# Two row tiles per visit in layer 1, and a reload in five parts

## The chip, the cores and the metric

The kernel runs on one core of one Trainium2 chip. The metric is the time of one execution on the device in microseconds (us), the median of several runs. A profile is one further execution, recorded instruction by instruction.

The core has engines that run side by side and wait for one another through semaphores. In the profile PE is the matrix array (PEld its weight loads), DVE the vector engine, ACT the scalar engine, POOL the general-purpose engine, and SP the engine that here only issues DMA transfers.

## The reference

Two layers of a graph network on 2708 nodes with 256 features. Layer 0 (top-p attention, two steps of neighbour averaging) is not touched by the change, except for where its result is kept. Layer 1 is graph attention with four heads of 64 features, followed by a residual and a layer norm:

```python
x = _layernorm(x + _L0_gnn_ref(x, adj, ...), axis=-1)
...
Wh = jnp.einsum('nd,hdo->nho', x, W)
s_i = jnp.einsum('nho,ho->nh', Wh, a_src)
s_j = jnp.einsum('nho,ho->nh', Wh, a_dst)
e = jax.nn.leaky_relu(s_i[:, None, :] + s_j[None, :, :], NEG_SLOPE)
adj_sl = adj.at[idx, idx].set(1.0)
mask = (adj_sl != 0)[:, :, None]
attention = jax.nn.softmax(jnp.where(mask, e, -jnp.inf), axis=1)
h_prime = jnp.einsum('ijh,jho->iho', attention, Wh)
x = _layernorm(x + h_prime.reshape(n, h * fo), axis=-1)
```

## The kernel before

The 2708 rows are cut into 22 row tiles: 16 of 128 rows and 6 of 110. Layer 1 takes its target rows in three groups (`spans`): tiles 0 to 7, 8 to 15, and 16 to 21. For each group it runs over all 22 source tiles, two at a time; `i` below is the place of a source tile in its group, 0 to 21, and `n` its place in the whole run of 66.

For one source tile and one group there are these steps.

- `mask` (line 245, by way of `neighbours` and `bars`): SP loads a block of the transposed adjacency matrix, 512 KB for a group of 1024 targets; ACT turns it into zeros and ones with Sign and Square (lines 247 and 248). DVE sets the diagonal where the source tile belongs to the group (line 251). Three such blocks are held. Within group 0 it also loads the source tile's values `v` (line 1594).
- `weights` (line 1606): for each of the four heads one DVE operation makes the unnormalised attention weights `pt` out of the targets' factors, the source's factor and the mask. There are three sets of `pt` (`DEEP`).
- `values` (line 1618) and `denominators` (line 1628): PE sums the weighted values and the weights themselves into PSUM. The array is split into four column strips of 32 (`SIDE`), so that four products run beside each other. The result stands transposed: features down, target rows across.

Two source tiles are summed together: values of both, then denominators of both. When a group is through, its sums are copied to `val` and `den`, and its tiles are put on the list `rest`. During the next group `beside(g, i)`, called before the values of each pair (even `i`) and again between values and denominators (odd `i`), takes work from that list. `settle` is a generator for one row tile. Its first step transposes the two halves of `val` and the denominators back with three full-array transposes into a PSUM tile `aux` (lines 1532 and 1533), takes the reciprocal on DVE (line 1535), and scales the four heads on ACT (line 1549). A later step adds the layer's input `xe` on POOL (line 1554). Then follow the layer norm on ACT and POOL (`layernorm_beside`, lines 149 to 157) and the store (line 1572, issued by ACT). `aux` has two buffers. Other users of `aux` are `share` (line 212), which turns the next group's target factors, at `i` = 11; `prepared` and `sources`, which finish the last three row tiles of layer 0 during group 0; and `verdict`, a test of layer 0's approximations whose sum (line 1481) falls into group 1. Group 2 is settled in `closing`, at the end.

`share` and `spread` send the factors through memory: SP stores one line (line 217, `shared<-line`), waits for it, and reads it back four times spread over all partitions (line 225, `r<-shared`).

Layer 0 writes its finished rows to memory (`xd`) as it goes, 19 tiles of them. The array `xe` in SBUF, in which layer 0 held something else, gets them back in group 0 of layer 1: at `i` = 12 POOL writes one column of all 19 tiles (line 1710), which SP's transfers wait for, and SP issues one transfer of 2 MB for tiles 0 to 15 and one of 330 KB for tiles 16 to 18 (line 1712). They are needed by the POOL adds of groups 1 and 2.

The order of PE, ACT, DVE and POOL in layer 1 is that of the program text. SP's order is left to the scheduler, which places each transfer by its own estimate.

```python
            if fast and (g, i) == (0, 12):
                nc.gpsimd.memset(xe[:, 0 : NT - LATE, 0:1], 0.0)
                for t0, t1 in ((0, 16), (16, NT - LATE)):
                    nc.sync.dma_start(
                        xe[: rows[t0], t0:t1, 0:D], xd[: rows[t0], t0:t1, :]
                    )
            if rest and i >= 2 and i % 2 == 0:
                running.append(settle(*rest.pop(0)[:4], aux(), False))
                next(running[-1])
```

Of the kernel before, what the change touches and what calls it, by code (L numbers as in the profile page):

```python
# [45 lines left out]
def kernel(  # L46
# [16 lines left out]
    nc = tc.nc  # L63
    N, D = x.shape
    DA = w1T.shape[1]
    STEPS = u1T.shape[0]
    H, _, FO = gat_w.shape
    DC = D // P
    NT = (N + P - 1) // P

    rows = [P] * 16 + [110] * 6
# [31 lines left out]
    xe = const.tile([P, NT, D + 2], F32, name="xe")  # L103
# [12 lines left out]
    xd = kept.tile([P, NT, D], F32, name="xd")  # L116
# [4 lines left out]
    LATE = 3  # L121
# [23 lines left out]
    def layernorm_beside(dst, src, m):  # L145

        col = {k: small.tile([P, 1], F32, name=f"lb_{k}")[:m] for k in ("nm", "sq", "rs", "nb")}
        nm, sq, rs, nb = col.values()
        nc.scalar.activation(dst, src, AF.Copy, accum_out=sq)
        nc.gpsimd.tensor_scalar(nm, sq, -1.0 / D, None, op0=ALU.mult)  # L150
        yield
        nc.scalar.activation(dst, src, AF.Square, bias=nm, accum_out=sq)
        nc.gpsimd.tensor_scalar(sq, sq, 1.0 / D, LN_EPS, op0=ALU.mult, op1=ALU.add)
        nc.gpsimd.tensor_tensor(rs, sq, minus_half[:m], op=ALU.pow)
        nc.gpsimd.tensor_mul(nb, nm, rs)
        yield
        nc.scalar.activation(dst, src, AF.Identity, scale=rs, bias=nb)
# [50 lines left out]
    def share(g, tr):  # L208

        span, m = spans[g], rows[spans[g][0]]  # L210
        k = len(span) * H
        nc.tensor.transpose(
            tr[:k, 0, :m],
            s_src[:m, span[0] : span[-1] + 1, :].rearrange("p t h -> p (t h)"), ident[:m, :m],
        )
        nc.scalar.activation(line[:k, :m], tr[:k, 0, :m], AF.Exp, scale=1.0 - NEG_SLOPE)
        nc.sync.dma_start(shared[g], line[:k, :m])

    def spread(g, r):

        lines = shared[g].rearrange("(t h) m -> h t m", h=H)
        n = len(spans[g]) * rows[spans[g][0]]
        for k in range(2):
            for h in range(2):
                nc.sync.dma_start(
                    r[k][:, h, :n].rearrange("p (t m) -> p t m", t=len(spans[g])),
                    lines[2 * k + h].partition_broadcast(P),
                )
# [25 lines left out]
    def room(pool):  # L254

        return [
            pool.tile([P, N], F32, name="e")[:, : 2 * GW].rearrange("p (h i) -> p h i", h=2)
            for _ in range(2)
        ]
# [1236 lines left out]
    def layer1(ep, adjp, r=None, verdict=None, early=()):  # L1496
# [27 lines left out]
        def aux():  # L1524
            return ps_u.tile([P, H, P], F32, name="aux")

        def settle(g, t, val, den, u, last):

            m = rows[t]
            cols = slice(off[t] - off[spans[g][0]], off[t + 1] - off[spans[g][0]])  # L1530
            for q in range(2):
                nc.tensor.transpose(u[:m, q, :], val[:, q, cols], ident)  # L1532
            nc.tensor.transpose(u[:m, 2, :], den[:, cols], ident)  # L1533
            rden = small.tile([P, H], F32, name="rden")
            nc.vector.reciprocal(  # L1535
                rden[:m], u[:m, 2, :].rearrange("p (h o) -> p h o", h=H)[:, :, 0]
            )
            res = pp.tile([P, H, FO], F32, name="res", bufs=5)
            sums = u[:m, 0:2, :].rearrange("p q (h o) -> p (q h) o", h=2)
            flat = res[:m].rearrange("p h o -> p (h o)")  # L1540
            if last and t % 2:
                for h in range(H):
                    nc.vector.scalar_tensor_tensor(  # L1543
                        res[:m, h, :], sums[:, h, :], rden[:m, h : h + 1],
                        xe[:m, t, h * FO : (h + 1) * FO], op0=ALU.mult, op1=ALU.add,
                    )
            else:
                for h in range(H):
                    nc.scalar.activation(
                        res[:m, h, :], sums[:, h, :], AF.Copy, scale=rden[:m, h : h + 1]  # L1550
                    )
            yield
            if not (last and t % 2):
                nc.gpsimd.tensor_add(flat, flat, xe[:m, t, 0:D])
                yield
            o = pp.tile([P, D], F32, name="o")[:m]
            if last:
                st = small.tile([P, 6], F32, name="ln_st")[:m]
                mv = small.tile([P, 2], F32, name="ln_mv")[:m]
                ve, rs, nb = (small.tile([P, 1], F32, name=f"ln_{k}")[:m] for k in ("ve", "rs", "nb"))  # L1560
                nc.vector.bn_stats(st, flat)  # L1561
                nc.vector.bn_aggr(mv, st)  # L1562
                nc.vector.tensor_scalar(ve, mv[:, 1:2], LN_EPS, None, op0=ALU.add)  # L1563
                nc.gpsimd.tensor_tensor(rs, ve, minus_half[:m], op=ALU.pow)  # L1564
                nc.gpsimd.tensor_scalar(nb, mv[:, 0:1], rs, -1.0, op0=ALU.mult, op1=ALU.mult)
                yield
                nc.scalar.activation(o, flat, AF.Identity, scale=rs, bias=nb)  # L1567
                nc.sync.dma_start(out[off[t] : off[t + 1], :], o)
                return
            yield from layernorm_beside(o, flat, m)  # L1570
            yield
            nc.scalar.dma_start(out[off[t] : off[t + 1], :], o)

        fast = r is not None
# [9 lines left out]
        for span in spans:  # L1584
            gw = off[span[-1] + 1] - off[span[0]]
            part = CHUNK if span is not spans[-1] else len(span) // 2 * rows[span[0]]
# [103 lines left out]
            yield from sources(t, pp, aux, nc.scalar)  # L1690


        late = []
        if verdict:
            late += [[2 * k, prepared(NT - LATE + k)] for k in range(LATE)]
            late.append([NT + 4, verdict(aux)])
        rest, running = [], []

        def beside(g, i):

            for part in list(late):
                if part[0] > 0:
                    part[0] -= 1
                elif next(part[1], late) is late:
                    late.remove(part)
            for part in list(running):
                if next(part, running) is running:
                    running.remove(part)
            if fast and (g, i) == (0, 12):
                nc.gpsimd.memset(xe[:, 0 : NT - LATE, 0:1], 0.0)  # L1710
                for t0, t1 in ((0, 16), (16, NT - LATE)):
                    nc.sync.dma_start(
                        xe[: rows[t0], t0:t1, 0:D], xd[: rows[t0], t0:t1, :]
                    )
            if rest and i >= 2 and i % 2 == 0:
                running.append(settle(*rest.pop(0)[:4], aux(), False))
                next(running[-1])
            if i == NT // 2 and g + 1 < len(spans):
                share(g + 1, aux())
                if g % 2:  # L1720
                    targets[g + 1] = room(ep)
                else:
                    targets[g + 1] = [rp.tile([P, 2, GW], F32, name=f"r{q}") for q in range(2)]
                spread(g + 1, targets[g + 1])
# [6 lines left out]
        for n in range(0, len(order), 2):  # L1731
            g, i, j = order[n]
            beside(g, i)
            weights(n + 2)
            mask(n + 3)
# [19 lines left out]
            if not last:  # L1755
                beside(g, i + 1)
# [3 lines left out]
            if last:  # L1760
# [4 lines left out]
                rest = [(g, t, val, den) for t in spans[g]]  # L1765
# [6 lines left out]
    with ExitStack() as both:  # L1772

        adjp = both.enter_context(tc.tile_pool(name="adjp", bufs=3))
        ep = both.enter_context(tc.tile_pool(name="ep", bufs=3))
        left = fast_layer0(ep, adjp)
        with tc.manual_schedule(engines=engines):
            layer1(ep, adjp, *left)
    flag = nc.values_load(bad[0:1, 0:1])
    with tc.If(flag > 0):  # L1780
        general_layer0()
        with ExitStack() as again:
            adjp = again.enter_context(tc.tile_pool(name="adjp", bufs=3))
            ep = again.enter_context(tc.tile_pool(name="ep", bufs=3))
            layer1(ep, adjp)
# [45 lines left out]
```

## Time and profile before

| | us |
|---|---|
| median of 3 runs | 1533.94 |
| lowest, highest | 1533.94, 1536.61 |
| profiled execution | 1534.79 |
| its span, first to last instruction | 1532.7 |
| PE busy over the span | 1492.8 |
| DVE busy | 1277.1 |
| ACT busy | 804.9 |
| POOL busy | 594.5 |

Layer 1 takes roughly the last 350 us. In a timeline a row gives the start and the length in us, the engine, the line, the operation with what it writes and reads, its shape and how many of them were put together; what stands in brackets is the idle time ahead of the row and what ended it. A PE row's length is modelled, so distances between starts say more than lengths. In a table of stretches each row gives a stretch, its length, the busy time (and number of instructions) of PE, PEld, DVE, ACT and POOL, the granted clock of PE, the busy share of the DMA engines, and GB/s.

### The profile page before, as it was taken

The page shows a single profiled execution, that of the slowest core. Times are in us where ns is not written, and L with a number is a line of the kernel's source. Part 1 is how long each engine was busy: PE and PEld are TensorE (multiplying, and loading weights), DVE is VectorE, ACT ScalarE, POOL GpSimd, SP SyncE. Part 2 cuts the span into 40 slices and gives each one's busy share as a digit, 9 for nine tenths or more (in the row PEclk, how much of TensorE's full clock was granted, in tenths as well). Part 3 has the DMA queues.
Part 4 walks back from the last instruction along what each step waited for, and adds up shares of the span by engine and source line. Part 5 has one row for each costly group of instructions (what it writes and reads, how often), then busy time and mean ns, then how long its engine had stood idle before and what let it go on. Part 6 is the DMA issues. An engine that isn't in the chain of part 4 may idle for free. (4 is left out here: it accounts for less than half of the span.)

```text
span 1532.7 us, 29967 instructions
## 1 busy us (share of the span) xinstructions
PE 1492.8 (97%) x10537; PEld 1064.6 (69%) x10537; DVE 1277.1 (83%) x3749; ACT 804.9 (53%) x1495; POOL 594.5 (39%) x959
## 2 busy tenths in 40 slices
PE   8999999999999999999999999999999999999996
PEld 4477777776778889988988888887898223433343
DVE  3699888999714978888889898989895998999996
ACT  3444444444326556655655666666653344456474
POOL 0046657566013323323454554544444310035143
PEclk9999999999999999999999999999999999999998
DMA  6288888878037755554564555555455355334331
GB/s 166 66 246 277 247 247 281 266 234 255 12 102 235 211 165 167 161 162 137 159 199 142 165 183 170 182 166 178 137 151 178 109 172 167 100 104 135 88 105 53
DMA packets 214488, 255.97 MB, mean 167 GB/s; under 512 B 42145, under 2 KB 180541, under 8 KB 214329
## 3 DMA queue, kind: packets, MB, share of 16 engines
q1 hardware_dynamic: 205622, 246.62, 53.7%
q10 hardware_dynamic: 8707, 7.35, 1.5%
q8 instruction: 85, 1.39, 0.4%
q14 instruction: 74, 0.61, 0.1%
HBM read 190.10 MB, written 62.44 MB: 165 GB/s over the span
## 5 line engine op out<-in xcount | busy, mean ns | idle before, releaser
L816 ACT ACTIVATE junk<-e,minus,rth 128x2708 bf16<-128x2708 f32 (+1 forms) x88 | 232.9, 2646 | 52.5 <-POOL rth L848 51.7
L271 ACT COPY eT<-tr 128x512 f32<-128x512 f32 (+5 forms) x264 | 141.5, 536 | 199.0 <-PE tr L266 196.5
L284 PE MATMUL att<-xm,eT 128*128 128x256 f32 (+3 forms) x968 | 230.8, 379 | 0.3 <-ACT xa L1325 0.3
L284 PE MATMUL att<-ba,eT 128*128 128x256 f32 (+3 forms) x968 | 230.9, 379 | 0.0
L1618 PE MATMUL acc<-pt,v 128*32 128x512 f32 (+3 forms) x2112 | 222.9, 543 | 2.1 <-DVE pt L1606 1.1
L1606 DVE SCALAR_TENSOR_TENSOR pt<-e,tj,blk 128x1024 f32<-128x1024 f32 (+3 forms) x176 | 186.6, 1125 | 8.3 <-ACT xw L1265 5.4
L284 PEld LDWEIGHTS att<-xm,eT 128*128 128x128 f32 (+3 forms) x968 | 169.6, 186 | 22.0 <-ACT xa L1325 0.7
L284 PEld LDWEIGHTS att<-ba,eT 128*128 128x128 f32 (+3 forms) x968 | 169.5, 186 | 22.0 <-ACT eT L271 0.8
L795 ACT ACTIVATE e<-lg 128x1024 f32<-128x1024 f32 (+1 forms) x132 | 121.0, 921 | 105.7 <-PE lg L791 102.2
L1109 PE MATMUL walk<-xe,blk 128*128 128x128 f32 (+3 forms) x1386 | 172.9, 275 | 1.2 <-ACT xw L1123 0.7
L1109 PEld LDWEIGHTS walk<-xe,blk 128*128 128x128 f32 (+1 forms) x1386 | 164.4, 187 | 11.4 <-issue 7.4
L1618 PEld LDWEIGHTS acc<-pt,v 128*32 128x32 f32 (+1 forms) x2112 | 73.4, 109 | 130.8 <-issue 76.2
L266 PE MATMUL tr<-ident,e 128*128 128x128 f32 (+3 forms) x968 | 147.5, 271 | 4.8 <-ACT eT L271 4.8
L266 PEld LDWEIGHTS tr<-ident,e 128*128 128x128 f32 (+3 forms) x968 | 111.3, 139 | 47.1 <-issue 26.7
L1109 PE MATMUL walk<-xm,blk 128*128 128x128 f32 (+3 forms) x1034 | 131.3, 277 | 5.4 <-DVE u_sb L1119 2.9
L1109 PEld LDWEIGHTS walk<-xm,blk 128*128 128x128 f32 (+3 forms) x1034 | 124.2, 188 | 14.0 <-issue 6.1
L1628 PE MATMUL acc<-pt,sb 128*32 128x512 f32 (+3 forms) x1056 | 115.7, 542 | 0.0
L1606 DVE SCALAR_TENSOR_TENSOR pt<-r,tj,blk 128x1024 f32<-128x1024 f32 (+1 forms) x88 | 109.9, 1312 | 1.3 <-issue 0.6
L247 ACT ACTIVATE blk<-blk 128x1024 f32<-128x1024 f32 (+3 forms) x66 | 63.3, 960 | 82.5 <-DMA blk<-in_adjT_dram 76.2
L896 DVE MAX8 cand<-e 128x8 f32<-128x170 f32 (+1 forms) x352 | 85.9, 320 | 21.1 <-ACT e L795 21.0
L896 DVE MAX8 cand<-scr 128x8 f32<-128x97 f32 (+1 forms) x616 | 102.8, 244 | 0.0
L914 DVE MAX8 top<-work 128x8 f32<-128x128 f32 (+3 forms) x242 | 82.3, 340 | 8.3
(283 smaller groups left out, 2410.2 us busy)
## 6 DMA issues: line engine op xcount, KB each, us to landing
blk<-in_adjT_dram SPq DMA_DIRECT2D x68, 512.0 KB
blk<-S SPq DMA_DIRECT2D x48, 512.0 KB
blk<-D SPq DMA_DIRECT2D x24, 512.0 KB
blk<-in_adjT_dram SPq DMA_DIRECT2D x26, 440.0 KB
D<-blk SPq DMA_DIRECT2D x16, 512.0 KB
S<-scr SPq DMA_DIRECT2D x16, 512.0 KB
S<-blk SPq DMA_DIRECT2D x16, 512.0 KB
xm<-S SPq DMA_DIRECT2D x16, 512.0 KB
```

The lines of the kernel that those rows point to most:

```text
L247: nc.scalar.activation(bar, bar, AF.Sign)
L266: nc.tensor.transpose(tr[: rows[t], q, :m], e[:m, off[t] : off[t + 1]], ident[:m, :m])
L271: copy(eT[:k, : len(grp), :m], tr[:k, : len(grp), :m])
L284: nc.tensor.matmul(acc, eT[: rows[t], q, :m], value(t), start=(t == 0), stop=(t == NT - 1),)
L795: nc.scalar.activation(halves[:m, :, c0 : c0 + w], lg[:m, :, :w], AF.Exp, accum_out=zp[:m, n : n + 1],)
L816: nc.scalar.activation(junk[:m], e[:m], func, scale=rth, bias=minus1[:m], accum_out=acc)
L896: nc.vector.max(cand[:, n, :], src[:m, n * size : min(N, (n + 1) * size)])
L914: nc.vector.max(top[:, k : k + 8], work if k else flat)
L1109: nc.tensor.matmul(ac, blk[:k, j, :], MOVING[name](j, k, w), start=start and j == 0, stop=j == PAIRS - 1, skip_group_check=True,)
L1606: nc.vector.scalar_tensor_tensor(pt[:k, :gw], targets[g][h // 2][:k, h % 2, :gw], tj[:k, j, h : h + 1], bar, op0=ALU.max, op1=ALU.mult,)
L1618: nc.tensor.matmul(acc[h // 2][c][to : to + SIDE, :w], v[j][:k, h, o : o + SIDE], probs[n][h][:k, c0 : c0 + w], **at,)
L1628: nc.tensor.matmul(acc[2][c][h * SIDE : (h + 1) * SIDE, :w], sb[:k, j, h : h + 1].to_broadcast([k, SIDE]), probs[n][h][:k, c0 : c0 + w], **at,
```

## The change

Two things are changed in `beside`. The reload of `xe` is cut into five parts, each with its own POOL write, placed at `i` = 12, 14, 16, 18 and 19 of group 0. And a visit for transposes takes two tiles from `rest` at `i` = 2, 6, 10 and 14, both with their own `aux` buffer, where before it took one at each even `i` from 2 to 16.

```diff
+        BACK = {12: (0, 4), 14: (4, 8), 16: (8, 12), 18: (12, 16), 19: (16, NT - LATE)}
         late = []
...
-            if fast and (g, i) == (0, 12):
-                nc.gpsimd.memset(xe[:, 0 : NT - LATE, 0:1], 0.0)
-                for t0, t1 in ((0, 16), (16, NT - LATE)):
-                    nc.sync.dma_start(
-                        xe[: rows[t0], t0:t1, 0:D], xd[: rows[t0], t0:t1, :]
-                    )
-            if rest and i >= 2 and i % 2 == 0:
-                running.append(settle(*rest.pop(0)[:4], aux(), False))
-                next(running[-1])
+            if fast and g == 0 and i in BACK:
+                t0, t1 = BACK[i]
+                nc.gpsimd.memset(xe[:, t0:t1, 0:1], 0.0)
+                nc.sync.dma_start(xe[: rows[t0], t0:t1, 0:D], xd[: rows[t0], t0:t1, :])
+            if rest and i % 4 == 2:
+                both = [settle(*rest.pop(0)[:4], aux(), False) for _ in rest[:2]]
+                for part in both:
+                    next(part)
+                running.extend(both)
```

## The prediction

> **What bounds the kernel now.** I read the page's engine table, then stretches of layer 1 (busy time of each engine), the timelines of PE, DVE, SP and ACT there, and the chain of waits. Layer 1 is 1186 us to the end. Its three groups of targets hold PE and DVE nearly full; two stretches (groups 1 and 2, closing left out) by PE, PEld, DVE, ACT, POOL:
>
> ```profile
> 1315.90:1435.23 119.33, 119.19 (x1086) 37.01 (x1082) 114.89 (x128) 65.89 (x122) 40.51 (x40) 1.00 0.39 111
> 1435.23:1507.80 72.57, 72.50 (x986) 33.69 (x982) 71.18 (x94) 48.12 (x111) 22.97 (x39) 1.00 0.35 96
> ```
>
> A PE that waits in its queue still counts as busy, so the period of a pair of source tiles tells more than the share. The PE timeline, start and length, with a visit (three transposes, L1532 and L1533) and without:
>
> ```profile
> 1393.39 7.07 PE L1618 MATMUL acc<-pt,v 128*32 128x512 f32 x64
> ...
> 1403.83 0.44 PE L1532 MATMUL aux<-ident,val 128*128 128x128 f32 x2
> 1404.10 0.27 PE L1533 MATMUL aux<-ident,den 128*128 128x128 f32 x1
> 1404.30 7.07 PE L1618 MATMUL acc<-pt,v 110*32 110x512 f32 x64
> ...
> 1414.63 7.05 PE L1618 MATMUL acc<-pt,v 110*32 110x512 f32 x64
> ```
>
> A pair with a visit takes 1404.30 - 1393.39 = 10.91 us, one without 10.33: the constant lengths show PE setting the pace in group 1. A visit costs 0.60 (10.91 less 10.31, the mean of the last pairs). In group 2 the same reading gives 7.29 and 6.70 (1494.43 to 1501.13). How much lies in the tiles and how much in going in and out shows where three tiles are turned in one visit, in the closing:
>
> ```profile
> 1514.99 0.43 PE L1532 MATMUL acc<-ident,val 128*110 128x128 f32 x2
> 1515.26 0.27 PE L1533 MATMUL acc<-ident,den 128*110 128x128 f32 x1
> 1515.37 0.38 PE L1532 MATMUL acc<-ident,val 128*110 128x128 f32 x2
> 1515.59 0.27 PE L1533 MATMUL acc<-ident,den 128*110 128x128 f32 x1
> 1515.69 0.38 PE L1532 MATMUL acc<-ident,val 128*110 128x128 f32 x2
> ```
>
> The second tile starts 0.38 after the first, the third 0.32 after the second (1515.69 - 1515.37). DVE is close behind in group 2; four masked products (L1606), reciprocal, four, four:
>
> ```profile
> 1456.56 3.74 DVE L1606 SCALAR_TENSOR_TENSOR pt<-e,tj,blk 128x660 f32<-128x660 f32 x4 [0.17 <-issue]
> 1460.22 0.17 DVE L1535 RECIPROCAL rden<-aux 128x4 f32<-128x4 f32 x1
> 1460.31 3.32 DVE L1606 SCALAR_TENSOR_TENSOR pt<-e,tj,blk 128x660 f32<-128x660 f32 x4
> 1463.84 3.84 DVE L1606 SCALAR_TENSOR_TENSOR pt<-e,tj,blk 128x660 f32<-128x660 f32 x4 [0.21 <-issue]
> ```
>
> DVE idles 0.2 in a period of 7.28, until the last denominators of the pair give their buffers back. From 1482 on the chain of waits leaves PE for DVE. The other half of the change is on SP. In group 0 one mask comes late:
>
> ```profile
> 1249.10 0.38 SPq L1712 DMA_DIRECT2D xe<-xd  x1
> 1252.23 0.33 SPq L245 DMA_DIRECT2D blk<-in_adjT_dram  x1
> 1252.61 0.38 SPq L1712 DMA_DIRECT2D xe<-xd  x1
> 1257.41 0.33 SPq L245 DMA_DIRECT2D blk<-in_adjT_dram  x1
> 1257.83 0.38 SPq L217 DMA_DIRECT2D shared<-line  x1
> 1263.07 6.37 SPq L225 DMA_DIRECT2D r<-shared  x4
> 1277.60 1.06 ACT L247 ACTIVATE blk<-blk 128x1024 f32<-128x1024 f32 x1 [8.14 <-DMA blk<-in_adjT_dram]
> 1280.03 1.14 PE L171 MATMUL aux<-wx,xT 128*110 128x264 f32 x4 [1.81 <-ACT xT L167]
> ```
>
> Behind it on ACT stands a copy (L167) that PE needs, and PE loses 1.81.
>
> **What the Trainium skill says.** "TensorEngine Tiling (Array Packing)", Key Properties: changing the tiling mode drains the array. The trace agrees: the sums run 128x32, the transposes 128x128, and 0.28 of a visit's 0.60 isn't transposes. "SBUF — State Buffer", SBUF: two separate sides: a DVE operation with two inputs in SBUF and a GpSimd operation that reads SBUF shut each other out. Here too: single products last 1.27, but 1.76 beside POOL's add (L1554). "DMA: Bandwidth & Descriptors", Queues, rings and completion order: a ring's descriptors are taken in order. The trace fits: the 16 KB of shared<-line, issued at 1257.83, held L225 until 1263.07, behind some 3.4 MB.
>
> **The change part by part.** *Visits.* Eight settled tiles in group 1 and eight in group 2 went out at i = 2, 4, ... 16; now two each at i = 2, 6, 10, 14. Eight visits vanish; their 24 transposes stay, at 0.11 each, 0.33 a tile (the closing's 0.32 rounded up).
> - Group 1: 4 x (0.60 - 0.33) = 1.1 off, if DVE keeps up. When PE reaches a product, DVE had it ready early; the smallest lead for the second tile of a pair (its third head) falls to 1.7 at i = 12. PE gains at most 0.83 on that point, so DVE stays ahead.
> - Group 2: 4 x (0.59 - 0.33) = 1.0 off PE. Two pairs take 14.31 instead of 14.57; DVE needs 2 x 7.08 = 14.2. It just holds, but two adds on POOL now fall into one pair: 2 x 0.48 on one pair's products eat half of a lead of 1.8. I charge 0.15 once, 0 to 0.5. At the end, where DVE leads, one L1554 add less stands beside it (the add of the visit at i = 16 hit 1501.00, 3.75 instead of 3.36): 0.2 back, 0 to 0.4.
> - New wait: both aux buffers are taken at once. At i = 11 of group 1 the verdict (L1481) and share (L212) want them back. Before, the reciprocal came at 1376.58, four activations (L1549, 0.93) ended at 1377.72, and PE arrived at 1378.11. Now eight end 0.93 later, 1378.65, less what DVE gains by then (0.28 by PE's start, 0.35 by an add moved): and 0.1 more for the second reciprocal: about 1378.1, with L212 due at 1378.0 (1378.23 - 0.55 for two visits saved + 0.33 for the double one). Behind it on PE stand that pair's denominators. I charge 0.2; 0 to 0.8.
> - ACT: eight activations in a row put the next mask back by 0.93. In group 2 it is ready some 6.2 after the pair's start, and DVE wants it at 6.8: nothing, but 0.3 a visit (1.2 in all) if ACT is later by 0.9. Reciprocals, adds, statistics and output DMAs are as many as before, in twos; o has two buffers, both DMAs leave one step before reuse, as now: nothing.
>
> *Reload.* By the instruction order of the changed kernel, POOL's five memsets stand back to back, none with a wait. SP isn't ordered by hand: its order becomes three parts, mask, two parts, mask, shared, four r, mask. So the reload is not spread over eight source tiles: it goes out as early as before. The same 2.4 MB and two masks lie ahead of shared, the same four r ahead of the late mask. Three issues more, 3 x 0.38 = 1.1 us, fall into SP's idle time (1249.5 to 1252.2, 1253 to 1257.4); four memsets of 0.13 at most follow the first, while POOL has 83 us free. The first of the two masks lands some 1.5 us earlier (512 KB less ahead at 350 GB/s, what the stretch from 1251 to 1257 moved): nobody waits, since DVE runs without a gap there. Cost 0; between -1.4 (the late mask in time) and +1.5 (SP held by r longer).
>
> Sum: -1.1 - 1.0 + 0.15 - 0.2 + 0.2 = -1.95, say -2.0. Profiled execution: 1534.79 (span 1532.7 and 2.1 around it) to 1532.8. It lies 0.85 over the median of the runs; taken from the median, 1533.94 - 2.0 = 1531.9.
>
> **Rivals.** (A) The late mask comes in time after all. For: it is the largest stall of layer 1, and smaller parts let something between. Against: shared waits behind the same bytes, r behind shared. Pair i = 14 would take 11.99 like pair 12, not 13.42: -1.4 more, -3.4, 1530.5.
> (B) DVE takes over. For: 71.18 of 72.57 us busy in group 2, from 1482 on the chain. Against: its idle 0.2 per pair is real. Group 2 gives nothing, group 1 half: -0.5, 1533.4.
> (C) Slower: r held up. In the instruction order each transfer waits for an earlier one that used the same of eight completion semaphores, and each r now waits for a smaller mask or reload part; if these finish after shared has landed, r and the late mask go back with them. For: the order names these waits. Against: SP takes a ring in order, and all were issued before shared. Every microsecond there is one on PE through L167 and L171; past 2.0 us it eats the gain, past 5.1 it shows as a loss. A whole reload (2.4 MB at 330 GB/s, 7 us) would give +5, 1538.9.
> That the reload isn't spread as the change says is part of my forecast, not a rival.
>
> **How the numbers follow.** Forecast 0.56, A 0.23, B 0.12, C 0.09. The bound for no change, 0.2% (3.1 us), is about what a measurement of this kernel can tell. The forecast's own range from its open costs is 1530.7 to 1533.3 (+1.4 with wait, mask and DVE bad; -1.2 with part of the late mask regained). With A whole, B and the runs' own spread: 1529.8 to 1534.2. Faster by over 0.2%: A and a seventh of the forecast, 0.31; within: 0.60; slower: C, 0.09.
>
> **What would show it.** Right: group 1's pairs alternate 11.25 (double visit) and 10.31, group 2's 7.6 and 6.7; group 2 starts 0.9 earlier against group 1's start; SP issues all five parts before 1254; L247 still waits about 8 us near 1277. Wrong: products of L1618 starting late in the pair after a double visit (B); that wait gone (A) or several us longer (C); L212 held over 0.8.

## The result, and the profile after

| | before | after |
|---|---|---|
| median of 10 runs, us | 1534.72 | 1540.24 |
| lowest, highest | 1533.46, 1536.65 | 1532.15, 1544.96 |
| profiled execution (span) | 1534.79 (1532.7) | 1537.19 (1535.4) |

The ratio is 1.0032, 95% interval 1.0021 to 1.0044: the change makes the kernel slower by 0.32%. Forecast was 1531.9.

Start where the forecast saw its gain. PE's timeline of the changed kernel shows the double visits, with the second tile 0.38 behind the first:

```profile
1325.30 0.44 PE L1532 MATMUL aux<-ident,val 128*128 128x128 f32 x2
...
1325.68 0.38 PE L1532 MATMUL aux<-ident,val 128*128 128x128 f32 x2
...
1326.10 7.08 PE L1618 MATMUL acc<-pt,v 128*32 128x512 f32 x64
1336.42 7.05 PE L1618 MATMUL acc<-pt,v 128*32 128x512 f32 x64
...
1347.64 7.07 PE L1618 MATMUL acc<-pt,v 128*32 128x512 f32 x64
...
1422.44 3.62 PE L1618 MATMUL acc<-pt,v 110*32 110x512 f32 x32
1426.85 5.07 PE L1618 MATMUL acc<-pt,v 110*32 110x512 f32 x30 [0.80 <-DVE pt L1606]
...
1434.76 0.73 PE L1618 MATMUL acc<-pt,v 128*32 128x330 f32 x4
...
1465.08 2.40 PE L1618 MATMUL acc<-pt,v 128*32 128x330 f32 x32
1469.15 3.48 PE L1618 MATMUL acc<-pt,v 128*32 128x330 f32 x30 [1.66 <-DVE pt L1606]
...
1475.87 4.65 PE L1618 MATMUL acc<-pt,v 128*32 128x330 f32 x64
```

The pair at 1326.10 takes 10.32, to 1336.42, and the next one, with a double visit behind it, 11.22, to 1347.64: 0.90 for a visit of two tiles, where two single visits took 1.20. But two pairs are broken in the middle. Half the products of the pair at 1422.44 are done by 1426.1, and the other half begins at 1426.85; that pair takes 12.32, to 1434.76, instead of 10.30. The pair at 1465.08, with a double visit behind it, takes 10.79, to 1475.87, instead of 7.59: its second half begins 4.07 after the first, not 2.2.

Here are the two stretches that the forecast showed of before, now of the changed kernel and between the same products. The columns are again the busy time of PE, PEld, DVE, ACT and POOL:

```profile
1314.12:1434.76 120.64, 119.34 (x1083) 38.57 (x1079) 114.78 (x128) 64.09 (x120) 48.75 (x40) 1.00 0.37 108
1434.76:1510.41 75.65, 73.71 (x991) 35.73 (x987) 69.85 (x95) 48.23 (x113) 35.77 (x40) 1.00 0.34 95
```

They are longer by 1.31 and 3.08. DVE is busy for less than before, and ACT for no more than 0.11 more. POOL is busy for more: 48.75 against 40.51 with the same 40 instructions, and 35.77 against 22.97 with 40 instead of 39. POOL's timeline shows which of them grew:

```profile
1408.94 11.76 POOL L153 TENSOR_SCALAR lb_sq<-lb_sq 128x1 f32<-128x1 f32 x1 [3.77 <-ACT o L152]
1420.79 0.57 POOL L154 TENSOR_TENSOR lb_rs<-lb_sq,minus_half 128x1 f32<-128x1 f32 x1
1421.44 0.19 POOL L155 TENSOR_TENSOR lb_nb<-lb_nm,lb_rs 128x1 f32<-128x1 f32 x1
...
1455.82 4.61 POOL L153 TENSOR_SCALAR lb_sq<-lb_sq 128x1 f32<-128x1 f32 x1 [2.73 <-ACT o L152]
```

L153 works on one number per partition. The longest one in groups 1 and 2 of before is this:

```profile
1357.03 1.67 POOL L153 TENSOR_SCALAR lb_sq<-lb_sq 128x1 f32<-128x1 f32 x1 [7.98 <-ACT o L152]
```

In the changed kernel one stands for 11.76 us. DVE in that time:

```profile
1403.84 16.82 DVE L1606 SCALAR_TENSOR_TENSOR pt<-r,tj,blk 110x1024 f32<-110x1024 f32 x14
1425.51 4.87 DVE L1606 SCALAR_TENSOR_TENSOR pt<-r,tj,blk 110x1024 f32<-110x1024 f32 x4 [4.85 <-ACT blk L248]
```

Fourteen products back to back, ending at 1420.66; L153 ends some 0.05 later. The one at 1455.82 ended at 1460.43, just after DVE began a reciprocal (1460.30), which reads PSUM, not two arrays in SBUF. A third one, of 3.10 at 1341.83, cost PE nothing. After its fourteen products DVE itself stands still for 4.85, waiting for a mask. ACT's timeline says why the mask is late:

```profile
1410.60 1.06 ACT L247 ACTIVATE blk<-blk 110x1024 f32<-110x1024 f32 x1 [1.25 <-DMA blk<-in_adjT_dram]
1411.69 1.06 ACT L248 ACTIVATE blk<-blk 110x1024 f32<-110x1024 f32 x1
1421.66 0.60 ACT L157 ACTIVATE o<-res,lb_nb,lb_rs 128x256 f32<-128x256 f32 x1 [8.91 <-POOL lb_nb L155]
1422.84 0.60 ACT L157 ACTIVATE o<-res,lb_nb,lb_rs 128x256 f32<-128x256 f32 x1 [0.58 <-POOL lb_nb L155]
1423.34 1.04 ACT L247 ACTIVATE blk<-blk 110x1024 f32<-110x1024 f32 x1
1424.42 1.06 ACT L248 ACTIVATE blk<-blk 110x1024 f32<-110x1024 f32 x1
```

ACT works in order. Its L157 scales a row tile by what L153 to L155 work out, so it stood for 8.91 us, and the mask of the next source tile stood behind it. That closes a circle: POOL waits for a break of DVE, ACT for POOL, the masks for ACT, and DVE makes no break until it runs out of masks. Before, the same wait of ACT reached 2.5 us at most (us in total, times, longest, from 1300 to 1520):

```profile
ACT o L157 <- POOL lb_nb L155: 7.5, 6, 2.5
```

After:

```profile
ACT o L157 <- POOL lb_nb L155: 23.1, 9, 8.9
...
DVE pt L1606 <- ACT blk L248: 9.3, 2, 4.9
```

The order of the reload was as forecast. SP issues all five parts within 5 us, with shared and r in their old places:

```profile
1247.88 1.48 SPq L1713 DMA_DIRECT2D xe<-xd  x3
1251.04 0.35 SPq L245 DMA_DIRECT2D blk<-in_adjT_dram  x1
1251.48 0.89 SPq L1713 DMA_DIRECT2D xe<-xd  x2
...
1256.66 0.38 SPq L217 DMA_DIRECT2D shared<-line  x1
1261.98 5.69 SPq L225 DMA_DIRECT2D r<-shared  x4
```

### The profile page after: what moved, and what is told of

Its sections match the earlier page's. It is cut to its first block, busy times and chain, and to the rows that moved or that the text cites. A ratio compares the mean times of both kernels' runs of the same rounds, so it can differ in the third digit from the quotient of the medians.

```text
span 1535.4 us, 30012 instructions
## 1 busy us (share of the span) xinstructions
PE 1492.7 (97%) x10537; PEld 1067.1 (70%) x10537; DVE 1275.3 (83%) x3749; ACT 802.5 (52%) x1495; POOL 614.9 (40%) x963
## 5 line engine op out<-in xcount | busy, mean ns | idle before, releaser
L1618 PE MATMUL acc<-pt,v 128*32 128x512 f32 (+3 forms) x2112 | 227.6, 544 | 5.1 <-DVE pt L1606 3.6
L1606 DVE SCALAR_TENSOR_TENSOR pt<-e,tj,blk 128x1024 f32<-128x1024 f32 (+3 forms) x176 | 185.2, 1120 | 12.1 <-ACT xw L1265 5.5
L1618 PEld LDWEIGHTS acc<-pt,v 128*32 128x32 f32 (+1 forms) x2112 | 76.2, 110 | 138.4 <-issue 77.0
L247 ACT ACTIVATE blk<-blk 128x1024 f32<-128x1024 f32 (+3 forms) x66 | 63.3, 961 | 102.1 <-DMA blk<-in_adjT_dram 93.5
L1606 DVE SCALAR_TENSOR_TENSOR pt<-r,tj,blk 128x1024 f32<-128x1024 f32 (+1 forms) x88 | 109.8, 1313 | 5.1 <-ACT blk L248 4.9
```

What stands on the lines that cost most here:

```text
L247: nc.scalar.activation(bar, bar, AF.Sign)
L1606: nc.vector.scalar_tensor_tensor(pt[:k, :gw], targets[g][h // 2][:k, h % 2, :gw], tj[:k, j, h : h + 1], bar, op0=ALU.max, op1=ALU.mult,)
L1618: nc.tensor.matmul(acc[h // 2][c][to : to + SIDE, :w], v[j][:k, h, o : o + SIDE], probs[n][h][:k, c0 : c0 + w], **at,)
```

## The experiments

The theory was: the double visits bunch the statistics of two tiles, POOL's small operations miss DVE's breaks, and ACT's in-order queue hands the delay to the masks. The rivals were: the reload costs; the double visits cost by themselves; what ACT does in twos costs, not POOL.

Whole runs are measured against runs of the kernel before on the same chip. They scatter by several us: the 41 to 59 runs of before lie within 6.4 to 8.8 us, so the spreads of under 3 or 4 us that some expectations name could decide nothing. Part of the scatter comes from stages that the change does not touch, since group 0 of layer 1 starts between 1183.95 and 1187.81 in the fourteen profiles. So the table also gives a length read from each profile, groups 1 and 2 from the first product of group 1 to the first product of group 2's pair `i` = 18, and the longest L153 of groups 1 and 2. What lies behind, from that pair to the end, takes 31.55 before, 31.89 after and 31.30 to 32.60 in the others.

| kernel | median, us | ratio, 95% interval | groups 1 + 2, us | longest L153, us |
|---|---|---|---|---|
| before | | | 119.76 + 65.90 = 185.66 | 1.67 |
| after | 1540.24 | 1.0032, 1.0021 to 1.0044 | 121.08 + 68.76 = 189.84 | 11.76 |
| reload_only | 1534.27 | 1.0004, 0.9995 to 1.0012 | 185.67 | 1.67 |
| pairs_only | 1539.46 | 1.0032, 1.0022 to 1.0041 | 189.64 | 11.79 |
| breaks | 1532.94 | 0.9992, 0.9985 to 0.9998 | 183.97 | 2.32 |
| stagger | 1532.75 | 0.9988, 0.9978 to 0.9998 | 183.62 | 1.47 |
| late_scale | 1530.81 | 0.9978, 0.9965 to 0.9990 | 183.80 | 11.83 |
| adds_together | 1533.98 | 0.9995, 0.9986 to 1.0003 | 183.80 | 2.46 |
| before_filled | 1534.90 | 1.0001, 0.9992 to 1.0010 | 186.10 | 1.67 |
| stagger_late | 1532.09 | 0.9985, 0.9975 to 0.9996 | 183.61 | 1.40 |
| before_late | 1532.47 | 0.9991, 0.9983 to 1.0000 | 185.66 | 1.67 |
| both_later | 1532.81 | 0.9992, 0.9984 to 1.0000 | 184.05 | 1.51 |
| late_breaks | 1530.78 | 0.9983, 0.9975 to 0.9991 | 183.90 | 2.06 |
| late_pairs | 1533.39 | 0.9991, 0.9981 to 1.0001 | 183.34 | 11.61 |

Below the first two rows, the first four kernels ran against 1533.69 (median of 59 runs of before), the next four against 1534.88 (47 runs), the last four against 1534.14 (41 runs).

### One half of the change each

reload_only keeps the five parts and takes one tile a visit as before; against the changed kernel:

```diff
-            if rest and i % 4 == 2:
-                both = [settle(*rest.pop(0)[:4], aux(), False) for _ in rest[:2]]
...
+            if rest and i >= 2 and i % 2 == 0:
+                running.append(settle(*rest.pop(0)[:4], aux(), False))
+                next(running[-1])
```

pairs_only keeps the double visits and takes the old reload:

```diff
-            if fast and g == 0 and i in BACK:
...
+            if fast and (g, i) == (0, 12):
...
```

> The reload of xe in five parts alone; visits with one tile as before. Theory (POOL starved by a DVE without breaks in groups 1 and 2, which the double visits bring): as before, within 0.1% (1533.5 to 1536), no wait of L157 for POOL over 2.5 us, pair i = 14 of group 0 some 0.6 us shorter than the 13.4 of before. Rival (the reload costs): 1537 or more, and a spread of over 5 us.

> Double visits alone; the reload in two parts as before. Theory (POOL starved): like the changed kernel, 1537 to 1542 with a spread of over 5 us between executions, and in the profile at least one L153 on POOL of over 3 us with L157, a mask and DVE waiting behind it. Rival (the reload costs): 1532 to 1533, two us under before, spread under 3 us.

The loss is that of the double visits alone: 1.0032 with the old reload, as with the new. POOL's timeline of pairs_only has the same hold-up at the same place, though group 0 went differently ahead of it:

```profile
1408.82 11.79 POOL L153 TENSOR_SCALAR lb_sq<-lb_sq 128x1 f32<-128x1 f32 x1 [3.74 <-ACT o L152]
...
1469.77 4.63 POOL L153 TENSOR_SCALAR lb_sq<-lb_sq 128x1 f32<-128x1 f32 x1 [1.89 <-ACT o L152]
```

### Breaks on DVE

The changed kernel with 22 writes of one number per partition put ahead of products on DVE, so that its row of two-input operations is interrupted.

```diff
                 bar = masks.pop(n)
+                if g and order[n][1] % 4 in (3, 0):
+                    nc.vector.memset(minus_half2, -0.5)
```

> The changed kernel with one tiny DVE operation that reads nothing (a memset of one column) put ahead of every other two source tiles' products in groups 1 and 2: 22 operations of about 0.1 us. Theory (POOL gets in only where DVE makes a break): the longest L153 falls to one source tile or two, under 6 us in group 1, DVE's waits for a late mask go, 1532 to 1534, spread under 4 us, though DVE has 2 us more to do. Rival (bunched work on ACT and output stores hold the masks): no better than the changed kernel, 1538 to 1543.

Groups 1 and 2 fall from 189.84 to 183.97, although DVE has more to do. POOL in the stretch of the long hold-up (L154 there is L153 of the others), and DVE (L1609 is L1606, and L1607 are the writes):

```profile
1409.19 2.32 POOL L154 TENSOR_SCALAR lb_sq<-lb_sq 128x1 f32<-128x1 f32 x1 [3.64 <-ACT o L153]
```

```profile
1404.21 8.46 DVE L1609 SCALAR_TENSOR_TENSOR pt<-r,tj,blk 110x1024 f32<-110x1024 f32 x7
1411.42 0.06 DVE L1607 MEMSET spare<- 128x1 f32 x1
```

11.76 has become 2.32: the operation is passed over at one boundary between products and ends at 1411.52, 0.04 after a write. By itself this run could also have helped by moving L153 in time, as the next ones do. But the ends of the hold-ups say the same everywhere. In groups 1 and 2 of the fourteen profiles, 14 of the 224 L153 last over 2 us, in seven kernels. Each of them ends within 0.06 us of the end of a DVE operation, where no product follows directly: DVE stands idle, or next is a reciprocal, one of these writes, or a small operation of `verdict`. So it is DVE's row of two-input products that keeps POOL out. That doing things in twos costs ACT too much is not what slowed the kernel, since ACT still does them in twos.

### The second tile later, and the two halves of what is bunched

stagger leaves the transposes of both tiles in one visit and lets the second tile's add and statistics start two calls of `beside` later:

```diff
+        def behind(part):
+            yield
+            yield
+            yield from part
...
-                running.extend(both)
+                running.extend((both[0], behind(both[1])))
```

adds_together has both adds together and only the second tile's statistics two calls later (`held` = 0 and 2). both_later has both statistics side by side, but one call later (`held` = 1 for both):

```diff
                 nc.gpsimd.tensor_add(flat, flat, xe[:m, t, 0:D])
                 yield
+                for _ in range(held):
+                    yield
```

> Double visits of PE and ACT as in the changed kernel, but the second tile's add, statistics and scaling come two calls later, where a single visit's would have stood. Theory: it depends on what made the breaks. If the two adds of one pair took DVE's breaks away, POOL gets them back: 1531.5 to 1533.5, spread under 4 us. If shorter pairs on PE did (DVE no longer waits for PE), it stays slow: 1537 to 1542. Rival (transposes in twos or the two aux buffers): slow, with L1532 or L212 waiting.

> The changed kernel with the two adds of a visit still together, but the second tile's statistics and scaling two calls later. If the two adds in one pair take DVE's breaks away (they cost DVE 2 x 0.48 in one pair), a long L153 stays: 1537 to 1542, spread over 5 us. If it is the bunched small operations on POOL, L153 stays under 2 us: 1531.5 to 1533.5.

> The changed kernel with the adds of both tiles where they were and the statistics of both tiles one call later, still side by side. If it is the two statistics side by side that miss the breaks: POOL's L153 is again held up for over 4 us somewhere in groups 1 and 2, ACT's L157 behind it, ratio 1.002 to 1.004. If the place in the pair decides (the call between values and denominators against the call before values): longest POOL row under 2.5 us, ratio 0.998 to 0.9995.

All three lose the long hold-up of L153, and groups 1 and 2 take 183.6 to 184.1. Not every operation of POOL gets in at once: in adds_together an L153 lasts 2.46, where under 2 was expected, and in both_later an L150, the first of the statistics, lasts 3.20 at 1341.72, where under 2.5 was expected for the longest of POOL. PE's pairs at these two places keep their length. So it isn't the two statistics side by side as such (both_later has them so), and not the two adds (adds_together). Where L153 comes to stand in time matters. That a row of products without a break isn't enough either is plain from stagger. DVE:

```profile
1395.57 24.83 DVE L1606 SCALAR_TENSOR_TENSOR pt<-r,tj,blk 110x1024 f32<-110x1024 f32 x20
```

POOL within that row:

```profile
1399.97 0.49 POOL L153 TENSOR_SCALAR lb_sq<-lb_sq 128x1 f32<-128x1 f32 x1 [5.60 <-ACT o L152]
1407.73 0.37 POOL L153 TENSOR_SCALAR lb_sq<-lb_sq 128x1 f32<-128x1 f32 x1 [1.99 <-ACT o L152]
1417.27 0.79 POOL L153 TENSOR_SCALAR lb_sq<-lb_sq 128x1 f32<-128x1 f32 x1 [3.96 <-ACT o L152]
```

Twenty products in a row, and three L153 got in within 0.8 us each.

### A full DVE without double visits

The first form of the theory was that saving PE time leaves DVE without breaks, and that this alone keeps POOL out. before_filled is the kernel before with a useless two-input product of 128 columns (0.28 us) ahead of each odd source tile's products in groups 1 and 2.

```diff
                 bar = masks.pop(n)
+                if g and order[n][1] % 2:
+                    nc.vector.tensor_tensor(spare, g_sb[:, 0:P], b_sb[:, 0:P], op=ALU.mult)
```

> The kernel before, single visits, with a useless product of two SBUF tiles (128 columns, about 0.28 us) put on DVE ahead of every odd source tile in groups 1 and 2, 22 of them, where DVE has 0.2 to 0.34 us of idle time a pair. Theory (a DVE without breaks starves POOL, whoever fills it): an L153 or L154 of over 3 us in the profile and a spread of over 5 us; the fill itself costs 0 to 4 us, so 1537 to 1546. Rival (it takes the double visits): no POOL operation over 2 us, 1534 to 1537, spread as before.

That form fell: no L153 over 1.67, and 1.0001. The added operation also makes boundaries of its own, so the run doesn't say that fullness is harmless everywhere; together with stagger it does say that it isn't enough.

### The road to PE: ACT's L157

late_scale is the changed kernel with L157 two calls later, and four buffers for `o` instead of two. POOL's and DVE's work stays where it was. The buffers were not tried alone; in the changed kernel ACT shows no idle time ahead of L149, the first to write an `o`.

```diff
         nc.gpsimd.tensor_mul(nb, nm, rs)
-        yield
+        for _ in range(1 + apart):
+            yield
         nc.scalar.activation(dst, src, AF.Identity, scale=rs, bias=nb)
```

> The changed kernel with ACT's last scaling (L157), which waits for POOL, two calls later (one pair of source tiles), and four o buffers so that this can be. POOL's work is the same. Theory: L153 is starved as before, or longer, but ends at the next visit's reciprocals, ahead of which no mask now waits: no wait of DVE for a mask over 2 us in groups 1 and 2, 1531.5 to 1533.5, spread under 4 us. Rival (bunched ACT work and stores): 1538 or more, since the same work stands in the same twos.

POOL's timeline of this run:

```profile
1408.51 11.83 POOL L153 TENSOR_SCALAR lb_sq<-lb_sq 128x1 f32<-128x1 f32 x1 [2.50 <-ACT o L152]
```

DVE's:

```profile
1395.45 24.84 DVE L1607 SCALAR_TENSOR_TENSOR pt<-r,tj,blk 110x1024 f32<-110x1024 f32 x20
1420.60 4.87 DVE L1607 SCALAR_TENSOR_TENSOR pt<-r,tj,blk 110x1024 f32<-110x1024 f32 x4 [0.31 <-ACT blk L249]
```

ACT's, where L158 is L157 of the others and L248 and L249 make the masks:

```profile
1415.08 1.06 ACT L248 ACTIVATE blk<-blk 110x1024 f32<-110x1024 f32 x1 [2.66 <-DMA blk<-in_adjT_dram]
1416.17 1.06 ACT L249 ACTIVATE blk<-blk 110x1024 f32<-110x1024 f32 x1
1418.87 0.75 ACT L248 ACTIVATE blk<-blk 128x660 f32<-128x660 f32 x1 [1.64 <-DMA blk<-in_adjT_dram]
1419.66 0.75 ACT L249 ACTIVATE blk<-blk 128x660 f32<-128x660 f32 x1
1421.97 0.60 ACT L158 ACTIVATE o<-res,lb_nb,lb_rs 128x256 f32<-128x256 f32 x1 [1.55 <-POOL lb_nb L155]
```

And PE's:

```profile
1411.76 7.05 PE L1619 MATMUL acc<-pt,v 110*32 110x512 f32 x64
1422.06 7.05 PE L1619 MATMUL acc<-pt,v 110*32 110x512 f32 x64
1432.36 5.29 PE L1619 MATMUL acc<-pt,v 128*32 128x330 f32 x62
```

This is the run that separates the links of the chain. POOL is held as long as ever, 11.83, under a row of the same length as in stagger, and L153 ends at 1420.34, in DVE's idle 0.31 after 1420.29. But the masks now stand ahead of L158, and PE keeps 10.30 a pair. Groups 1 and 2 take 183.80, 1.86 less than before. Of this hold-up nothing reaches the end; the circle was closed by L157. The hold-up of group 2 did not come in this profile; late_pairs below has it.

The control, before_late, is the same edit to the kernel before, one tile a visit.

> The kernel before (one tile a visit, reload in two parts) with the scaling on ACT (L157) two calls later, four buffers for o. If what late_scale gained over before comes from the saved visits, and moving the scaling only takes away the stall that the double visits bring: here 1.000, within 0.998 to 1.001 of before, since before ACT waited at L157 2.5 us at most. If the late scaling gains by itself (masks that come earlier on ACT): 0.998, as late_scale, and the visits would be worth nothing.

Its groups 1 and 2 take 185.66, as before to the hundredth. The median is 0.09% lower, and the interval just reaches 1; the difference can't come from these groups. So late_scale's gain there is that of the visits.

### Cures together, and what is fastest

stagger_late is stagger with the late scaling, late_breaks is breaks with it, and late_pairs is pairs_only with it.

> Double visits, second tile's add and statistics two calls later (stagger) and ACT's scaling two calls later with four o buffers (late_scale). Theory: both cures together, no stall left: 1531 to 1532.5, spread under 3 us, faster than before by 0.1 to 0.2%. Rival: same as stagger.

> The changed kernel with both cures: scaling two calls later, and small DVE writes before products in groups 1 and 2. If the scaling on ACT is the only road by which POOL's delay reaches PE: nothing more than late_scale, ratio 0.9978 plus the DVE time of the breaks in group 2 (0.5 to 1 us), 0.998 to 0.9985; POOL's longest row falls under 2.5 us. If POOL's delay costs on another road too (stores, o buffers): faster than late_scale, 0.997.

> Double visits and late scaling with the old reload in two parts. If the reload in five parts is worth nothing: same as late_scale, 0.9975 to 0.9985 of before. If it gained or cost something that the stall covered in the other pairs of runs: 0.05% or more from late_scale, to either side.

Nothing is left for a second cure to gain: 183.61, 183.90 and 183.34 in groups 1 and 2, against 183.80 for late_scale. late_pairs repeats late_scale's finding with the other reload, and more strongly: L153 is held for 11.61, and in group 2 twice more, for 4.70 and 4.53, and yet PE's pairs up to `i` = 16 are even but for one that takes 7.68 instead of 7.59. Its ratio is 0.13% above late_scale's, with overlapping intervals. In its profile pair `i` = 14 of group 0, where the late mask is, takes 15.16. With the two-part reload this pair took 12.35 to 15.16 in five profiles (mean 13.47), with the five-part one 12.32 to 13.56 in nine (mean 12.87). A gain of some 0.6 us by the reload can be neither claimed nor excluded.

late_scale (1530.81) and late_breaks (1530.78) have the lowest times, both with intervals wholly below 1: faster than the kernel before by about 0.2%, and faster than the changed one by about 0.5%. The intervals of breaks, stagger and stagger_late also lie below 1 and overlap with these two, so which of the five is fastest is not settled. Of the 0.22% of late_scale, 3.4 us, groups 1 and 2 show 1.86; the rest is not shown to come from the change, since before_late, too, whose groups 1 and 2 take as long as before, reads 0.09% lower.

## Why the prediction was wrong

- **Visits: right.** A double visit costs 0.90 against twice 0.60; 11.22 was forecast as 11.25, and 7.59 as 7.6. Wherever the hold-up is out of the way, groups 1 and 2 are 1.6 to 2.3 shorter than before, against 1.75 by the sum's terms for that stretch. The 0.2 that the end was to give back did not come: from pair `i` = 18 of group 2 to the end, the kernels with double visits take 31.72 to 32.60, before 31.55. One reading of the sum was off without harm: at `i` = 12 of group 1 the smallest lead of DVE was that of the fourth head, 0.9, not the third's 1.7. DVE stayed ahead there even so.
- **The wait of L212: right in kind, small in size.** Pair `i` = 10 with `share` takes 10.81; 0.51 above a plain pair, against 0.35 before (11.26 with a visit of 0.60 in it, 10.91 without). That is 0.16, and 0.2 was charged. Pair 12 lost another 0.3 (11.52 instead of 11.22) that no term had and whose cause is open.
- **Reload: right** that it is not spread, and 0 is within what the runs can tell (reload_only 1.0004, 0.9995 to 1.0012). L247 near 1277 still waits 7.54, against 8.14.
- **The step that failed** is "Reciprocals, adds, statistics and output DMAs are as many as before, in twos; o has two buffers, both DMAs leave one step before reuse, as now: nothing". Their number is the same, but not when they get through. The prediction named the lock between DVE and POOL, showed it in the trace, and charged it to DVE alone (0.15 for two adds). The other direction, POOL kept out by DVE, was not priced, and no reason was given. It cost 6.0: 189.84 against 183.80. With -1.86 for the visits that is +4.18 in groups 1 and 2, and the medians differ by +5.5. The profiled run of the changed kernel, 1537.19, is one of its faster ones, so in a typical run the hold-ups may well cost more than 6.0; that is not shown.
- **ACT was priced with the wrong quantity.** The 0.93 of four more activations put the masks back, as forecast, at no cost. The 8.91 that one ACT instruction waits for POOL had no term. The rule that the prediction applied to PE's L212, ask who stands behind the waiting instruction, would have found the masks behind L157.
- **Rivals.** A did not come: pair 14 took 12.82, not 11.99. B did not: DVE is busy for less of group 2 than before. The sign named for B, products of L1618 starting late, did appear (1426.85 and 1469.15), but what came late was a mask for DVE. C was on the right side for a reason that did not occur: r was issued at 1261.98, 5.3 after shared, 5.2 before. So the 0.09 given to "slower" was right by luck only.

There was a warning in the trace of before that the prediction does not use, in group 0, on POOL's timeline:

```profile
1224.44 5.23 POOL L1681 TENSOR_TENSOR ln_rs<-ln_ve,minus_half 110x1 f32<-110x1 f32 x1 [4.92 <-DVE ln_ve L1680]
```

The same operation takes 0.55 in the closing, with DVE not in its way (L1564). One that lasts 5.23 is not working but waiting. The trace shows no engine that waits for this one, so it cost nothing there.

Not settled: why L153 misses every boundary from 1408.94 on and gets in within one or two in stagger and both_later. A break is not always needed: the L1681 above missed three boundaries and came through in the middle of a row of products. The runs rule out fullness alone and bunching alone. Single runs of the changed kernel reach from 1532.15 to 1544.96, wider than before's; that would fit a hold-up whose length changes from run to run, but only one run of it was profiled.

## What to carry to other kernels

When small operations of one engine are regrouped, count not only how many there are but how long each can be kept from starting, and follow the in-order queue of whoever waits for them to the first instruction that the bottleneck needs. Where such an instruction is not urgent, put it behind the urgent ones: moving one scaling two steps later was worth 0.5%, and the hold-up itself could stay. A circle of waits (here POOL, ACT, DVE) shows up as a tiny operation with a long duration, so sort the small shapes by duration before trusting that they cost nothing.

## What the runs showed of the hardware that was not expected

- The Trainium skill, "SBUF — State Buffer", SBUF: two separate sides, says that of a DVE operation with two SBUF inputs and a GpSimd operation that reads SBUF the one that starts first has the ports for the whole instruction, and the other blocks. The traces agree in kind, but the blocked one is not sure of the next turn: L153 missed nine boundaries between DVE products that follow one another every 1.2 us, 11.76 in all, and ended within 0.1 us of DVE stopping (1420.66 and 1420.70; 1420.29 and 1420.34 in late_scale).
- Most get in soon: 210 of the 224 L153 last under 2 us, such as the 0.37, 0.49 and 0.79 in stagger, under a row of 20 products that left no gap.
- 22 one-number writes on DVE went with a longest wait of 2.32 (2.06 in late_breaks), and cost nothing that groups 1 and 2 show (183.97 against 183.62 to 184.05 in the three runs with shifted statistics). Behind them breaks takes 32.60 to the end, but late_breaks, with the same writes, 31.75.
